# Where pieces of VectorE and ScalarE work end in the list of work of a two-layer perceiver kernel

## The chip, the cores and the metric

The kernel runs on one core of one Trainium2 chip. The metric is the device time of one launch in microseconds (us), the median of several runs. A profiled execution of the kernel gives the durations below; it is one execution, with a time of its own.

## What is computed

The input x has 16 sequences of 64 tokens of 256 numbers; a context has 16 sequences of 1601 rows of 256. Six blocks follow each other, each on a normed x and added to it (types are float32 throughout):

```
x = x + cross_attention_0(layernorm(x), ctx)       # softmax(QK/16) V, then an output matrix
x = x + self_attention(layernorm(x))               # 16 heads of 16, low rank, q and k normed by their root mean square, causal
x = x + tiled_ffn(layernorm(x))                    # one of 8 matrices by position
x = x + cross_attention_1(layernorm(x), ctx)
x = x + state_space(layernorm(x))                  # convolution, softplus time steps, scan over 64 tokens, gate
x = x + experts(layernorm(x))                      # 8 of 64 experts a token, plus one shared
```

layernorm is (x - mean) / sqrt(var + 1e-5) over the 256 numbers.

## The kernel before, in words

The 1024 tokens lie in SBUF as 8 groups g of 128 (two sequences each). The blocks are folded into one program with these stages:

- **Attention stage.** chain(g) does for one group the query and cross attention of layer 0 ("a"), mla (self attention), ffn, and cross attention of layer 1 ("b"). Before a cross, turn_ctx transposes the context of a sequence (on TensorE, copied to cT). At the end prepare_ssm loads and transposes W_in for the next block.
- **State space and routing stage.** inlet(g) makes the convolution and its transposes, sums(lo, hi) the softplus and its segment sums, which go through DRAM (segd), scan(g) the scan, route(g) the choice of experts; the chosen rows are scattered by GpSimd into a table in DRAM, xbuf, sorted by expert.
- **Expert stage.** Rows come back by quads of experts (L1442), pass up and down, and are scattered by GpSimd into a second table in DRAM, ybuf, one row for each token and choice (L1481). At the end each group reads its 8 rows a token from ybuf (L1555) and sums them with their weights.

**What sets the order.** The stages are generators, and drive (a planner in the program text) lets several run at once: two chains at a time, and beside them one prepare_ssm, two inlets, one sums. Each `yield cost, gap` tells the planner that the step just written takes TensorE `cost` us and that the generator should not go on for `gap` us more; the planner takes the first generator whose time has come. A third word may stand there: "want" asks for the one slot for attention scores, "free" gives it up. The order of the text so made is a priority for the framework that builds the program: it puts the instructions of each engine in an order of its own, by when they become ready and by that priority, and each engine executes its own order strictly.

Places that the change and the later steps touch:

- layernorm, L199 to L214: bn_stats (L201), bn_aggr (L203) and the sum with epsilon ve (L205) on VectorE, the power -0.5 rs on GpSimd (L207), the apply xn on VectorE (L213). All are written at once, and after it the caller yields (0, 2.7) or the like. In query of layer a, `beside` is turn_ctx of the group's first context: its seven steps stand between the norm and the transposes of xn.
- turned, L658: two transposes of xn, then a copy of them (xnT) by evac, L190, which takes VectorE (L195) and ScalarE (L197) in turns over all its calls.
- cross, L562: scores in four pieces j (L576), each with its maximum (L583); exponentials on ScalarE (L597), then `yield 0.3, 2.0, "free"`. After it come the sum and its reciprocal (L601, L603), turn(j), which transposes a piece (L612) and copies it to paT by evac, and weigh, the product with the context (L620).
- mla, L742: products with q and k weights (mq, L753) and their squares on ScalarE (L754); the root of the mean square on VectorE, one sum, two small operations and three rounds of three (L757 to L767), and q and k times it (mqk, L773). Then a copy of xnT by GpSimd (L780), v (mv, L783), its masked form vb (L785), transposes and keys (L796 to L806), "want", and the scores in four tiles pss (L819). The softmax runs in two halves i, both written in one step: mask added (L830, two), maximum (L837), difference (L838), exponential mee on ScalarE (L840). After the two halves `yield 1.2, 3.8, "free"`, then transposes (L846), copies (L848) and the product with v (L856).
- clear, L183: called by chain(g) after mla(g); two transfers on SP's queue that wait for mla's last product write an eighth of xbuf (L185) and an eighth of ybuf (L187) with zeros from a small tile, each row in two halves of 136 or 128 numbers. load_ctx (L379, L380) and W_in's tiles wl (L997, L1000) use the same queue.
- sums, L309: softplus in some 24 small VectorE operations (L320 to L338) around one exponential (L322), written in one step.
- inlet, ffn and route call layernorm as the others do.

Of the kernel before, what the change touches and what calls it, by code (L numbers as in the profile page):

```python
# [10 lines left out]
F32 = mybir.dt.float32  # L11
I32 = mybir.dt.int32
# [6 lines left out]
P = 128  # L19
# [128 lines left out]
def perceiver_kernel(ctx: ExitStack, tc: tile.TileContext, a: dict, consts: bass.AP, out: bass.AP):  # L148
# [28 lines left out]

    zero = cst.tile([P, DX // 2], F32, name="zero")
    G.memset(zero, 0.0)
    xbuf0 = xbuf.rearrange("(p n) (c d) -> p (n c) d", p=P, c=2)  # L180
    ybuf0 = ybuf.rearrange("(p n) (c d) -> p (n c) d", p=P, c=2)

    def clear(lo, hi, stage):  # L183

        after(nc.sync.dma_start(out=xbuf0[:, 2 * lo : 2 * hi, :], in_=_bc(zero, 1, 2 * (hi - lo))), [stage])  # L185
        lo, hi = (n * NTOK * TOPK // NSLOT for n in (lo, hi))
        after(nc.sync.dma_start(out=ybuf0[:, 2 * lo : 2 * hi, :], in_=_bc(zero[:, 0 : D // 2], 1, 2 * (hi - lo))), [stage])  # L187

# [9 lines left out]

    def layernorm(src, name, xn, parted=False):  # L199
        st = small.tile([P, 6], F32, tag="ln_st", name=f"st_{name}")  # L200
        V.bn_stats(st, src)  # L201
        mv = small.tile([P, 2], F32, tag="ln_mv", name=f"mv_{name}")
        V.bn_aggr(mv, st)  # L203
        ve = small.tile([P, 1], F32, tag="ln_ve", name=f"ve_{name}")
        V.tensor_scalar(ve, mv[:, 1:2], 1e-5, None, ALU.add)  # L205
        rs = small.tile([P, 1], F32, tag="ln_rs", name=f"rs_{name}")
        G.tensor_tensor(rs, ve, neghalf[:, 0:1], ALU.pow)  # L207
        if parted:

            src, to = src.rearrange("p (k c) -> p k c", c=2), xn.rearrange("p (c k) -> p k c", c=2)  # L210
        else:
            to = xn
        V.tensor_scalar(to, src, mv[:, 0:1], rs, ALU.subtract, ALU.mult)  # L213
        return xn  # L214

# [51 lines left out]
    def inlet(g, tile1, tile2):  # L267
        yield from until(lambda: "winT" in sw)
        xnT, winT = sw["xnT"], sw["winT"]
        tk = slice(g * P, (g + 1) * P)  # L270
        xn = layernorm(x[:, g, :], f"ss{g}", tile1([P, D], f"xn_ss{g}"))
        yield 0, 2.8
        pt = pst([P, 2, P], f"psx_ss{g}")
# [35 lines left out]
    def sums(lo, hi):  # L309
# [11 lines left out]
        u = sp("u")  # L321
        A.activation(u, na, AF.Exp)  # L322
        up2 = sp("up2")
        V.tensor_scalar(up2, u, 2.0, None, ALU.add)
# [8 lines left out]
        for k in range(13, 0, -2):  # L333
            V.tensor_tensor(po, po, r2, ALU.mult)
            V.tensor_scalar(po, po, 2.0 / k, None, ALU.add)
        V.tensor_tensor(po, po, r, ALU.mult)
        dt = sp("dt")
        V.scalar_tensor_tensor(dt, dv, 0.0, po, ALU.max, ALU.add)  # L338
        yield 0, 4.0
        sg = sw["pool"].tile([n, (NL + 1) * P], F32, tag="sg", name=f"sg_{lo}")  # L340
# [10 lines left out]
    with ExitStack() as p1:  # L351
# [181 lines left out]
        def query(g, lay, beside=None):  # L533
# [3 lines left out]
            xs = x[:, g, :]  # L537
            xn = layernorm(xs, f"xa{nm}", tile1([P, D], f"xn_{nm}"))
            if beside:
                yield from beside  # L540
            else:
                yield 0, 2.7
            xnT = turned(xn, f"xa{nm}")
# [18 lines left out]
        def cross(g, lay):  # L562
# [31 lines left out]
            for j in range(4):  # L594
# [3 lines left out]
                pas.append(pa)  # L598
            yield 0.3, 2.0, "free"
            sm = small.tile([P, 1], F32, tag="sm", name=f"sm_{nm}")  # L600
# [141 lines left out]
        def mla(g):  # L742
            wqk, wvo, wkr, vbs = wts["m"]
            xs = x[:, g, :]
            xn = layernorm(xs, f"ml{g}", tile1([P, D], f"xn_ml{g}"))
            yield 0, 2.7
            xnT = turned(xn, f"ml{g}")
# [3 lines left out]
            for c in range(2):  # L751
# [3 lines left out]
                pqs.append(pq)  # L755
            ms = small.tile([P, 32], F32, tag="mms", name=f"mms_{g}")
            V.reduce_sum(ms, sq.rearrange("p c (n d) -> p (c n) d", d=HD), AX.X)  # L757
            me = small.tile([P, 32], F32, tag="mme", name=f"mme_{g}")
            V.tensor_scalar(me, ms, 1.0 / HD, EPS_RMS, ALU.mult, ALU.add)

            rr = small.tile([P, 32], F32, tag="mrr", name=f"mrr_{g}")
            V.tensor_scalar(rr.bitcast(I32), me.bitcast(I32), -0.5, 1597463007.0, ALU.mult, ALU.add)
            for i in range(3):
                t = small.tile([P, 32], F32, tag="mt", name=f"mt_{g}_{i}")
                V.tensor_tensor(t, rr, rr, ALU.mult)
                V.scalar_tensor_tensor(t, t, -0.5, me, ALU.mult, ALU.mult)
                V.scalar_tensor_tensor(rr, t, 1.5, rr, ALU.add, ALU.mult)  # L767
            qk = tile2([P, 2, 2, P], f"mqk_{g}")
            for c in range(2):
                pv = pqs[c].rearrange("p (j n d) -> p j n d", j=3, d=HD)  # L770
                rv = rr.rearrange("p (c j n) -> p c j n", c=2, j=2)
                for j in range(2):
                    V.tensor_tensor(  # L773
                        qk[:, c, j, :].rearrange("p (n d) -> p n d", d=HD), pv[:, 2 * j, :, :], _bc(rv[:, c, j, :], 2, HD), ALU.mult
                    )
            yield 0.7, 0.1
            vs = []
            for c in range(2):
# [12 lines left out]
                vs.append(vb)  # L791
            yield 0.9, 5.0
            ptq = pst([P, 2, P], f"mtq_{g}")
# [22 lines left out]
            for c in range(2):  # L816
                for r in range(4):
                    for b in range(2):
                        T.matmul(  # L819
                            pss[r][b * 64 : (b + 1) * 64, c, :],  # L820
                            lhsT=qT[r * 32 : (r + 1) * 32, c, b * 64 : (b + 1) * 64],
                            rhs=kbs[c][r * 32 : (r + 1) * 32, b, :, :].rearrange("p h k -> p (h k)"),
                            start=True,
                            stop=True,
                        )
            ees, eTs = [], []
            for i in range(2):
# [13 lines left out]
                ees.append(ee)  # L841
            yield 1.2, 3.8, "free"
            for i in range(2):
# [87 lines left out]
        def ffn(g):  # L931
            fw, ohb, fb = wts["f"]
            xs = x[:, g, :]
            xn = layernorm(xs, f"ff{g}", tile1([P, D], f"xn_ff{g}"))
            yield 0, 2.7
            xnT = turned(xn, f"ff{g}")
# [192 lines left out]
    def route(g):  # L1129
# [5 lines left out]
        tk = slice(g * P, (g + 1) * P)  # L1135
        layernorm(x[:, g, :], f"mo{g}", xr[:, g, :], parted=True)
        yield 0, 2.8 if g == NG - 1 else 5.0
        pt = pst([P, 2, P], f"psx_mo{g}")
# [497 lines left out]
```

## Time and profile before

| | us |
|---|---|
| runs, device time | 1113.68, 1114.81, 1122.16 |
| median | 1114.81 |
| profiled execution, device time | 1104.11 |
| its span, first to last instruction | 1102.2 |

| stage (us from the span's start) | TensorE busy | VectorE busy | ScalarE busy | GpSimd busy | granted clock |
|---|---|---|---|---|---|
| 0 to 602, attention | 495.8 | 290.8 | 150.7 | 44.0 | 0.92 |
| 602 to 644, inlets | 26.2 | 30.5 | 18.2 | 8.2 | 0.80 |
| 644 to 890, scan and routing | 202.7 | 182.2 | 51.7 | 126.8 | 0.76 |
| 890 to 1062, experts | 159.2 | 68.4 | 50.6 | 91.5 | 0.96 |
| 1062 to 1102, sum of the rows | 17.3 | 18.5 | 0.0 | 3.9 | 0.78 |

The granted clock is TensorE's, as a share of full speed. In the profile's lines PE is TensorE, PEld its weight load, DVE VectorE, ACT ScalarE, POOL GpSimd, SPq the DMA queue of SyncE; L12 is line 12 of the kernel, and the names are those of the program, out<-in. In a timeline a line begins with its start and its duration in us; what stands in brackets at its end is the idle time of the engine before it and what ended that. A wait for several things is put down to the one that came last.

### The profile page before, as it was taken

The page shows a single profiled execution, that of the slowest core. Times are in us where ns is not written, and L with a number is a line of the kernel's source. Part 1 is how long each engine was busy: PE and PEld are TensorE (multiplying, and loading weights), DVE is VectorE, ACT ScalarE, POOL GpSimd, SP SyncE. Part 2 cuts the span into 40 slices and gives each one's busy share as a digit, 9 for nine tenths or more (in the row PEclk, how much of TensorE's full clock was granted, in tenths as well). Part 3 has the DMA queues.
Part 4 walks back from the last instruction along what each step waited for, and adds up shares of the span by engine and source line. Part 5 has one row for each costly group of instructions (what it writes and reads, how often), then busy time and mean ns, then how long its engine had stood idle before and what let it go on. Part 6 is the DMA issues. An engine that isn't in the chain of part 4 may idle for free. (4 is left out here: it accounts for less than half of the span.)

```text
span 1102.2 us, 16572 instructions
## 1 busy us (share of the span) xinstructions
PE 901.2 (82%) x6242; PEld 684.8 (62%) x6242; DVE 590.5 (54%) x1823; ACT 271.2 (25%) x592; POOL 274.4 (25%) x326
## 2 busy tenths in 40 slices
PE   4887889978799788979867569999999449999955
PEld 3665656645656456556554458888888338888834
DVE  1346454356545554364535874976867773343316
ACT  0213132321332222331313543222210013233310
POOL 0000101001000001001010222266665524655650
PEclk7878998989999899999978878887867669999988
DMA  6411324303613307103430073544411877989336
GB/s 235 172 38 62 100 89 130 120 2 99 184 36 120 97 4 219 59 2 100 103 91 11 28 153 84 118 113 113 113 42 41 277 263 241 304 282 296 116 119 269
DMA packets 99511, 138.99 MB, mean 126 GB/s; under 512 B 10211, under 2 KB 85407, under 8 KB 96358
## 3 DMA queue, kind: packets, MB, share of 16 engines
q1 hardware_dynamic: 84816, 116.36, 34.8%
q0 software_dynamic: 7680, 17.33, 4.6%
q10 hardware_dynamic: 6934, 4.23, 1.5%
q8 instruction: 50, 0.82, 0.3%
q14 instruction: 31, 0.25, 0.1%
HBM read 97.54 MB, written 44.53 MB: 129 GB/s over the span
## 5 line engine op out<-in xcount | busy, mean ns | idle before, releaser
L1481 POOL DMA_INDIRECT ybuf<-yo,goal x96 | 93.5, 974 | 81.3 <-ACT yo L1507 32.7
L1473 PE MATMUL ps_ee<-xT,wq 128*128 128x192 f32 x512 | 96.1, 331 | 0.0
L1115 POOL DMA_INDIRECT xbuf<-xtok,idx x64 | 70.0, 1094 | 71.3 <-DVE idx L1205 48.1
L1473 PEld LDWEIGHTS ps_ee<-xT,wq 128*128 128x128 f32 x512 | 82.5, 191 | 6.5 <-issue 5.0
L620 PE MATMUL po_a<-cn,paT_a 128*64 128x256 f32 (+1 forms) x416 | 59.5, 424 | 22.6 <-ACT mee L840 19.2
L207 POOL TENSOR_TENSOR rs_ff<-ve_ff,neghalf 128x1 f32<-128x1 f32 x8 | 4.4, 548 | 219.1 <-DVE ve_ff L205 211.6
L946 PE MATMUL fpy<-fw,fxm 128*128 128x256 f32 x256 | 58.3, 387 | 0.7 <-DVE fxm L943 0.7
L1337 PEld LDWEIGHTS ps_g<-pc,pb 64*128 64x128 f32 x768 | 51.8, 207 | 10.4 <-issue 5.1
L620 PE MATMUL po_b<-cn,paT_b 128*64 128x256 f32 (+1 forms) x416 | 51.2, 395 | 7.9 <-DVE paT_b L195 4.5
L1337 PE MATMUL ps_g<-pc,pb 64*128 64x64 f32 x768 | 54.7, 295 | 3.0 <-DVE zt L1326 2.0
L620 PEld LDWEIGHTS po_a<-cn,paT_a 128*64 128x64 f32 (+1 forms) x416 | 31.0, 150 | 40.9 <-ACT mee L840 20.1
L946 PEld LDWEIGHTS fpy<-fw,fxm 128*128 128x128 f32 x256 | 49.3, 196 | 8.8 <-PE py_a L654 2.2
L391 PE MATMUL psc<-ct,cn 128*128 128x128 f32 x384 | 52.3, 289 | 2.8 <-DVE cc_a L558 2.8
L391 PEld LDWEIGHTS psc<-ct,cn 128*128 128x128 f32 x384 | 46.9, 150 | 6.6 <-DVE cc_a L558 3.1
L576 PE MATMUL sc_a<-cT,qT_a 128*64 128x512 f32 (+1 forms) x256 | 48.7, 521 | 0.0
L1461 PE MATMUL ps_xT<-ct,xg 128*128 128x128 f32 x192 | 30.9, 289 | 19.7 <-DMA xg<-xbuf 19.7
L1323 POOL TENSOR_TENSOR pc<-cT,e 128x256 f32<-128x256 f32 x48 | 36.1, 787 | 39.3 <-ACT cT L1306 39.3
L1347 DVE COPY_PREDICATED gt<-ct,ps_g 128x256 f32<-128x256 uint32 x96 | 42.3, 545 | 5.2 <-PE ps_g L1337 5.2
L576 PE MATMUL sc_b<-cT,qT_b 128*64 128x512 f32 (+1 forms) x256 | 44.7, 501 | 0.4
L197 ACT COPY cT<-psc 128x512 f32<-128x512 f32 x48 | 28.0, 589 | 66.5 <-PE psc L391 66.5
L620 PEld LDWEIGHTS po_b<-cn,paT_b 128*64 128x64 f32 (+1 forms) x416 | 28.8, 141 | 24.9 <-DVE paT_b L195 5.5
L1475 ACT ACTIVATE hg<-ps_ee 128x192 f32<-128x192 f32 x64 | 21.2, 331 | 93.6 <-PE ps_ee L1473 90.9
(430 smaller groups left out, 1831.9 us busy)
## 6 DMA issues: line engine op xcount, KB each, us to landing
cn<-in_ctx_dram SPq DMA_DIRECT2D x16, 1536.0 KB
e<-segd SPq DMA_DIRECT2D x16, 896.0 KB
xbuf<-zero SPq DMA_DIRECT2D x8, 1632.0 KB
xg<-xbuf SPq DMA_DIRECT2D x16, 816.0 KB
ybuf<-zero SPq DMA_DIRECT2D x8, 1024.0 KB
wq<-in_L_ffn_We_gate_dram SPq DMA_DIRECT2D x16, 512.0 KB
wq<-in_L_ffn_We_up_dram SPq DMA_DIRECT2D x16, 512.0 KB
wq<-in_L_ffn_We_down_dram SPq DMA_DIRECT2D x16, 512.0 KB
```

The source lines that it names most:

```text
L197: A.copy(dst, src)
L391: T.transpose(ps[:, j, :], cn[:, 4 * q + j, c * P : (c + 1) * P], ident)
L576: T.matmul(sc[b * 64 : (b + 1) * 64, :], lhsT=qT[:, c, b * 64 : (b + 1) * 64], rhs=cTs[2 * g + b][:, c, 512 * j : 512 * j + n], start=c == ...
L620: T.matmul(po[b * 64 : (b + 1) * 64, :], lhsT=paTs[j][:, i, b * 64 : (b + 1) * 64], rhs=cns[2 * g + b][0:r, k, :], start=k == 0, stop=k == KC,
L946: T.matmul(py, lhsT=xm[:, t, c, :], rhs=fw[:, 2 * h + t, c, :], start=h + t + c == 0, stop=h == 3 and t == 1 and c == 1,)
L1115: sct = G.indirect_dma_start(out=xbuf, out_offset=bass.IndirectOffsetOnAxis(ap=idx[:, g, k : k + 1], axis=0), in_=xtok[:, g, 0:DX], in_off ...
L1323: G.tensor_tensor(pc[:, l, :, :].rearrange("p j (k h) -> p j k h", h=1 << l), half(cT, l, 1), half(ev, l, 1), ALU.mult)
L1337: T.matmul(pgs[q][:, i, j, :], lhsT=pb[q * 64 : (q + 1) * 64, l + i, j, :], rhs=pc[q * 64 : (q + 1) * 64, l + i, j, :], start=True, stop=True,
L1347: V.copy_predicated(gt.rearrange("p (j q) (k u h) -> p q j k u h", q=2, u=2, h=h)[:, q, :, :, 1, :], _bc(lvl[:, l + i, :].rearrange("p (k ...
L1461: T.transpose(to, xgs[q][:, 2 * part + s, c * P : (c + 1) * P], ident)
L1473: T.matmul(pe[:, j, :], lhsT=w, rhs=xTs[q][:, i, c, :], start=c == 0, stop=c == 1)
L1481: arr = G.indirect_dma_start(out=ybuf, out_offset=bass.IndirectOffsetOnAxis(ap=goal, axis=0), in_=y, in_offset=None, bounds_check=NTOK * T ...
```

## The change

- layernorm becomes a generator. After rs it yields (0, 1.8), or, where `beside` is given, three steps of it; then the apply is written, and then the rest of `beside`. The callers yield (0, 0.9) behind it instead of (0, 2.7) (route: 1.0 or 3.2 instead of 2.8 or 5.0).
- mla: v and vb are written ahead of the root; yields stand between the root and mqk, between the scores and the softmax, and between the softmax's halves. The score slot is given up after the second half, as before.
- cross: copies of the pieces go to VectorE for even j and to ScalarE for odd j; the yield before them is (0.35, 2.4).
- sums: three yields more.
- clear: xbuf is cleared with whole rows of 272 numbers; ybuf is not cleared.

```diff
-    zero = cst.tile([P, DX // 2], F32, name="zero")
+    zero = cst.tile([P, DX], F32, name="zero")
     G.memset(zero, 0.0)
-    xbuf0 = xbuf.rearrange("(p n) (c d) -> p (n c) d", p=P, c=2)
-    ybuf0 = ybuf.rearrange("(p n) (c d) -> p (n c) d", p=P, c=2)
+    xbuf0 = xbuf.rearrange("(p n) d -> p n d", p=P)
     def clear(lo, hi, stage):
-        after(nc.sync.dma_start(out=xbuf0[:, 2 * lo : 2 * hi, :], in_=_bc(zero, 1, 2 * (hi - lo))), [stage])
-        lo, hi = (n * NTOK * TOPK // NSLOT for n in (lo, hi))
-        after(nc.sync.dma_start(out=ybuf0[:, 2 * lo : 2 * hi, :], in_=_bc(zero[:, 0 : D // 2], 1, 2 * (hi - lo))), [stage])
+        after(nc.sync.dma_start(out=xbuf0[:, lo:hi, :], in_=_bc(zero, 1, hi - lo)), [stage])
...
-    def layernorm(src, name, xn, parted=False):
+    def layernorm(src, name, xn, parted=False, beside=None):
...
         G.tensor_tensor(rs, ve, neghalf[:, 0:1], ALU.pow)
+        if beside is None:
+            yield 0, 1.8
+        else:
+            for _ in range(3):
+                yield next(beside)
...
         V.tensor_scalar(to, src, mv[:, 0:1], rs, ALU.subtract, ALU.mult)
-        return xn
+        if beside is not None:
+            yield from beside
...
@@ sums
         A.activation(u, na, AF.Exp)
+        yield 0, 1.2
...
             V.tensor_scalar(po, po, 2.0 / k, None, ALU.add)
+            if k in (9, 5):
+                yield 0, 1.2
...
-        yield 0, 4.0
+        yield 0, 1.5
@@ query, and likewise inlet, mla, ffn and route without beside
-            xn = layernorm(xs, f"xa{nm}", tile1([P, D], f"xn_{nm}"))
-            if beside:
-                yield from beside
-            else:
-                yield 0, 2.7
+            xn = tile1([P, D], f"xn_{nm}")
+            yield from layernorm(xs, f"xa{nm}", xn, beside=beside)
+            if not beside:
+                yield 0, 0.9
@@ cross
-            yield 0.3, 2.0, "free"
+            yield 0.35, 2.4, "free"
...
-                evac(paT, pt)
+                (A.copy if j % 2 else V.tensor_copy)(paT, pt)
@@ mla
                 pqs.append(pq)
-            ms = small.tile([P, 32], F32, tag="mms", name=f"mms_{g}")
...
-                    V.tensor_tensor(
-                        qk[:, c, j, :].rearrange("p (n d) -> p n d", d=HD), pv[:, 2 * j, :, :], _bc(rv[:, c, j, :], 2, HD), ALU.mult
-                    )
-            yield 0.7, 0.1
+            yield 1.0, 0
             vs = []
...
                 vs.append(vb)
-            yield 0.9, 5.0
+            yield 0.9, 0.3
+            ms = small.tile([P, 32], F32, tag="mms", name=f"mms_{g}")
...
+                V.scalar_tensor_tensor(rr, t, 1.5, rr, ALU.add, ALU.mult)
+            yield 0, 2.8
+            qk = tile2([P, 2, 2, P], f"mqk_{g}")
...
+            yield 0, 1.2
             ptq = pst([P, 2, P], f"mtq_{g}")
...
+            yield 0.7, 0.2
             ees, eTs = [], []
...
                 ees.append(ee)
-            yield 1.2, 3.8, "free"
+                yield (0, 2.0) if i == 0 else (0, 1.0, "free")
             for i in range(2):
...
-                yield 0.55, (1.3, 0.7)[i]
+                yield 0.55, (1.5, 0.7)[i]
```

More of the change, by code (lines that the diff above doesn't have):

```diff
@@ L270, in inlet @@
         tk = slice(g * P, (g + 1) * P)
-        xn = layernorm(x[:, g, :], f"ss{g}", tile1([P, D], f"xn_ss{g}"))
-        yield 0, 2.8
+        xn = tile1([P, D], f"xn_ss{g}")
+        yield from layernorm(x[:, g, :], f"ss{g}", xn)
+        yield 0, 0.9
         pt = pst([P, 2, P], f"psx_ss{g}")
@@ L537, in query @@
             xs = x[:, g, :]
-            xn = layernorm(xs, f"xa{nm}", tile1([P, D], f"xn_{nm}"))
-            if beside:
-                yield from beside
-            else:
-                yield 0, 2.7
+            xn = tile1([P, D], f"xn_{nm}")
+            yield from layernorm(xs, f"xa{nm}", xn, beside=beside)
+            if not beside:
+                yield 0, 0.9
             xnT = turned(xn, f"xa{nm}")
@@ L744, in mla @@
             xs = x[:, g, :]
-            xn = layernorm(xs, f"ml{g}", tile1([P, D], f"xn_ml{g}"))
-            yield 0, 2.7
+            xn = tile1([P, D], f"xn_ml{g}")
+            yield from layernorm(xs, f"ml{g}", xn)
+            yield 0, 0.9
             xnT = turned(xn, f"ml{g}")
@@ L755, in mla @@
                 pqs.append(pq)
-            ms = small.tile([P, 32], F32, tag="mms", name=f"mms_{g}")
[L757 to L772, printed above, removed]
-                    V.tensor_tensor(
-                        qk[:, c, j, :].rearrange("p (n d) -> p n d", d=HD), pv[:, 2 * j, :, :], _bc(rv[:, c, j, :], 2, HD), ALU.mult
-                    )
-            yield 0.7, 0.1
+            yield 1.0, 0
             vs = []
@@ L791, in mla @@
                 vs.append(vb)
-            yield 0.9, 5.0
+            yield 0.9, 0.3
+            ms = small.tile([P, 32], F32, tag="mms", name=f"mms_{g}")
+            V.reduce_sum(ms, sq.rearrange("p c (n d) -> p (c n) d", d=HD), AX.X)
+            me = small.tile([P, 32], F32, tag="mme", name=f"mme_{g}")
+            V.tensor_scalar(me, ms, 1.0 / HD, EPS_RMS, ALU.mult, ALU.add)
+            rr = small.tile([P, 32], F32, tag="mrr", name=f"mrr_{g}")
+            V.tensor_scalar(rr.bitcast(I32), me.bitcast(I32), -0.5, 1597463007.0, ALU.mult, ALU.add)
+            for i in range(3):
+                t = small.tile([P, 32], F32, tag="mt", name=f"mt_{g}_{i}")
+                V.tensor_tensor(t, rr, rr, ALU.mult)
+                V.scalar_tensor_tensor(t, t, -0.5, me, ALU.mult, ALU.mult)
+                V.scalar_tensor_tensor(rr, t, 1.5, rr, ALU.add, ALU.mult)
+            yield 0, 2.8
+            qk = tile2([P, 2, 2, P], f"mqk_{g}")
+            for c in range(2):
+                pv = pqs[c].rearrange("p (j n d) -> p j n d", j=3, d=HD)
+                rv = rr.rearrange("p (c j n) -> p c j n", c=2, j=2)
+                for j in range(2):
+                    V.tensor_tensor(
+                        qk[:, c, j, :].rearrange("p (n d) -> p n d", d=HD), pv[:, 2 * j, :, :], _bc(rv[:, c, j, :], 2, HD), ALU.mult
+                    )
+            yield 0, 1.2
             ptq = pst([P, 2, P], f"mtq_{g}")
@@ L933, in ffn @@
             xs = x[:, g, :]
-            xn = layernorm(xs, f"ff{g}", tile1([P, D], f"xn_ff{g}"))
-            yield 0, 2.7
+            xn = tile1([P, D], f"xn_ff{g}")
+            yield from layernorm(xs, f"ff{g}", xn)
+            yield 0, 0.9
             xnT = turned(xn, f"ff{g}")
@@ L1135, in route @@
         tk = slice(g * P, (g + 1) * P)
-        layernorm(x[:, g, :], f"mo{g}", xr[:, g, :], parted=True)
-        yield 0, 2.8 if g == NG - 1 else 5.0
+        yield from layernorm(x[:, g, :], f"mo{g}", xr[:, g, :], parted=True)
+        yield 0, 1.0 if g == NG - 1 else 3.2
         pt = pst([P, 2, P], f"psx_mo{g}")
```

## The prediction

> **What bounds the kernel now.** I read the page's slices first, then the busy time by stage, then the waits of TensorE up to 602 us, and last the timeline around each long wait.
>
> ```profile
> PE   4887889978799788979867569999999449999955
> PEclk7878998989999899999978878887867669999988
> ```
>
> No engine is full from end to end. By stage (busy time by windows): four fifths of the attention stage, 0 to 602 us, is TensorE work (495.8 us); the short stage from 602 to 644 us is VectorE (30.5 of 42 us, TensorE 26.2); 644 to 890 us is TensorE (202.7) and VectorE (182.2) together; 890 to 1062 us is TensorE alone (159.2 of 172). The change lies almost wholly in the first stage, so what counts there is when TensorE stands still:
>
> ```profile
> PE po_a L620 <- ACT mee L840: 19.2, 4, 4.8
> PE pq_a L550 <- DVE xnT_xaa L195: 8.5, 3, 3.1
> PE ps_win L1041 <- DMA wl<-in_L_attn_W_in_dram: 7.8, 1, 7.8
> ```
>
> The columns are total us, times, longest. Three causes, eight stalls, 35.5 us. The timeline of the first (one of four alike, near 105, 235, 363 and 491 us):
>
> ```profile
> 363.62 0.68 DVE L837 TENSOR_REDUCE mmx<-ms 128x8 f32<-128x512 f32 x1
> 364.32 0.69 DVE L838 TENSOR_TENSOR ms<-ms,mmx 128x512 f32<-128x512 f32 x1
> 364.93 0.75 DVE L830 TENSOR_TENSOR ms<-ms,ct 128x256 f32<-128x256 f32 x2
> 365.72 0.69 DVE L837 TENSOR_REDUCE mmx<-ms 128x8 f32<-128x512 f32 x1
> 366.44 0.69 DVE L838 TENSOR_TENSOR ms<-ms,mmx 128x512 f32<-128x512 f32 x1
> 367.05 0.68 DVE L195 COPY paT_a<-pspa_a 128x512 f32<-128x512 f32 x1
> 367.88 3.40 PE L620 MATMUL po_a<-cn,paT_a 128*64 128x256 f32 x16 [4.81 <-ACT mee L840]
> ```
>
> The reader is to see a queue. TensorE ended the transposes pspa_a at 363.07; the copy paT_a that the next matmuls need was therefore ready to start. It stood on VectorE behind both halves of self attention's softmax and ran at 367.05. The wait is booked to ScalarE's mee only because that ended at about the same time.
>
> The second cause (three times, near 164, 294 and 421 us) is a norm in front of a copy:
>
> ```profile
> 164.50 0.15 DVE L205 TENSOR_SCALAR ve_ff<-mv_ff 128x1 f32<-128x1 f32 x1
> 165.38 0.80 DVE L213 TENSOR_SCALAR xn_ff<-x,mv_ff,rs_ff 128x256 f32<-128x256 f32 x1 [0.73 <-POOL rs_ff L207]
> 166.10 0.41 DVE L195 COPY xnT_xaa<-psx_xaa 128x256 f32<-128x256 f32 x1
> 166.57 2.07 PE L550 MATMUL pq_a<-xnT_xaa,pr_A 128*128 128x128 f32 x8 [2.70 <-DVE xnT_xaa L195]
> ```
>
> VectorE waits 0.73 us for the power on GpSimd, applies the norm, and only then copies what TensorE has waited for since 163.87. The third is a transfer behind a transfer on SP's queue:
>
> ```profile
> 547.22 4.83 SPq L187 DMA_DIRECT2D ybuf<-zero  x1
> 552.10 5.70 SPq L1000 DMA_DIRECT2D wl<-in_L_attn_W_in_dram  x4
> 559.21 1.94 PE L1041 MATMUL ps_win<-ct,wl 128*128 128x128 f32 x8 [7.83 <-DMA wl<-in_L_attn_W_in_dram]
> ```
>
> One more thing must be known: the order on an engine is not the order in which the code is written. Inside one step of mla the copies of the other chain stand between the steps of the root:
>
> ```profile
> 351.70 0.18 DVE L765 TENSOR_TENSOR mt<-mrr 128x32 f32<-128x32 f32 x1
> 351.80 0.69 DVE L195 COPY cT<-psc 128x512 f32<-128x512 f32 x1
> 352.40 0.18 DVE L766 SCALAR_TENSOR_TENSOR mt<-mt,mme 128x32 f32<-128x32 f32 x1
> ```
>
> So the builder already fills holes, and what a yield changes is which of two ready instructions goes first. That is just what fails in the first two causes.
>
> **The change part by part.** *Self attention's softmax, and the engines of the copies.* By the yields: the crossing chain ends its scores at t, gives up its slot at t+0.35 and turns its first piece at t+2.75. mla issues its scores at t+0.35, half 0 at t+1.25, half 1 at t+3.25, which the 0.55 of turn(0) pushes to 3.3. The order becomes half 0, paT of piece 0 on VectorE, half 1; piece 1 goes to ScalarE, where in time it is ready before half 1's exponential. In the trace's times: L830 twice ends at 361.36, mmx and ms of half 0 (0.68 + 0.69) at 362.8, the sum sm_a waits as now for the exponentials until 363.54 and with the reciprocal ends at 363.9, the copy (0.68) at 364.6, TensorE starts at 364.7 instead of 367.88: 3.2 us, four times, **-12.8**. What is late next is half 1: its exponential ends about 367.2 (364.6 + 0.75 + 0.69 + 0.69 + 0.63), about as now (367.85), so mla's own chain loses nothing by this sum. The copies themselves: piece 3 was copied by VectorE for layer b (L195 paT_b, mean 480 ns, two forms) and now goes to ScalarE, with the 512-wide pieces shared; 8 x (687 - 290) ns = 3.2 us more on VectorE and less on ScalarE, in a stage where VectorE is busy 290.8 of 602 us: nothing on the path. Mla now keeps the score slot until half 1 is issued, 2.9 of planned time instead of 1.2. Who waits for that? The next cross scores (L576) start 34 to 36 us after mla's scores (L819) in every pair I looked at (101.5 to 138.0, 147.2 to 181.0, 360.0 to 395.2): nobody.
>
> *Self attention's root.* mv and vb are issued ahead of it and the root is cut from mqk. At 349.7 to 355 us the two already stand mixed and TensorE is full (9.98 of 10 us): 0. Uncovered, it could move mqk by two vb, 0.84 us, on eight mla.
>
> *Norms.* L213 is issued 1.8 of planned time later. Near 164 us the copy xnT_xaa can then follow ve_ff directly at 164.65 and ends at 165.06 instead of 166.51: 1.45 us, three times, **-4.4**. The apply then waits for rs_ff to 165.34 as before and is at most 0.1 us later. Other norms: xtok L213 leaves VectorE idle 19.0 us in all for rs_mo in the scan stage (a reading of the groups), where copies into gt could go first; TensorE's waits for psx_mo there are only 8 us in all, so I take **-2** between 0 and -8. In the last route the apply could be late by one small operation: +0.2 us, up to +1.
>
> *Zeros of ybuf.* Eight transfers of 1024 KB go. Between 550 and 558 us the engines moved 284 to 333 GB/s, so 1.05 MB is 3.5 us; the clear of xbuf with rows of 1088 bytes instead of two of 544 is worth up to 1 us. [...] I take 0.7. Seven of the eight clears are hidden: TensorE waits for no cn at all in the list. The eighth stands in front of wl: wl lands 4.2 us earlier, and the 7.83 us stall becomes 3.6: **-4.2**. If prepare_ssm should issue those wl ahead of the clear, more; if later work stops TensorE there instead, 0.
>
> *Softplus.* Same instructions, three places to be interrupted, planned 1.1 longer in sum. Its two uses bound a TensorE wait of 3.77 us (L343 on sp_dt, near 658) and lie beside VectorE-bound conv work (9.76 and 9.62 of 10 us from 610 to 630): 0, between -3 and +3.
>
> *The clock.* After long stalls the granted clock is 0.5. Windows behind the stalls show it:
>
> ```profile
> 364.00:371.00 7.00, 3.12 (x16) 1.91 (x16) 3.66 (x8) 1.74 (x3) 0.00 (x0) 0.51 0.00 0
> 166.00:173.00 7.00, 6.43 (x29) 6.32 (x30) 2.90 (x7) 1.23 (x3) 0.76 (x2) 0.51 1.11 295
> 294.00:301.00 7.00, 3.85 (x31) 3.62 (x31) 4.42 (x11) 1.36 (x4) 1.97 (x3) 1.00 1.10 303
> ```
>
> (The seventh number is the clock.) TensorE work under the slow clock behind the stalls: 17.5 us behind the four softmax stalls, 9.7 behind two of the three norms, 2.9 behind wl; together 30 us, half of it lost, 15 us. [...] The rows do not agree: a stall of 2.70 us (163.87) was followed by the slow clock and one of 3.15 us (294.05) was not. Since 1.67 us more of idleness stands just ahead of each softmax stall, I take half: **-7.5**, ends 0 and -15.
>
> *Against it.* Every step of mla is now open to the other chain, and TensorE executes in order, so a step placed too early blocks it. By the sum above half 1's exponential ends at 367.2 and its transposes (L846) come up on TensorE at about 367.3: no margin. I take 1 us for each of eight mla: **+8**, between 0 and +36 (see below).
>
> Sum: -12.8 - 4.4 - 2 + 0.2 - 4.2 - 7.5 + 8 = -22.7. The profiled execution took 1104.11 us (span 1102.2 and 1.9 around it), so 1081.4. The median of the runs shown is 1114.81, 1.0097 times that; 1081.4 x 1.0097 = **1091.9**, say 1092.
>
> **The rivals.** *Only the zeros count (0.2).* The builder fills holes by itself, so the finer steps merely exchange one copy for another, and the four stalls of 4.8 us come back elsewhere. For it: the mixed order shown above. Against it: the copy paT_a was ready and still went last. Then -4.2 and a little clock, -1.4: 1098.5, as a median 1109.
>
> *Everything comes (0.08).* No new stall and the whole clock: -12.8 - 4.4 - 4 - 4.2 - 15 = -40: 1064, as a median 1074.
>
> *The stall moves to half 1 (0.12), slower.* TensorE reaches L846 of half 1 before its exponential. A full half and its exponential cost 0.75 + 0.69 + 0.69 + 0.63 = 2.8 us, and 3.4 us of slow clock behind it lose 1.7: 4.5 on eight mla is +36; the softmax gain is then void, with norms and zeros -8.6 kept: +27, 1131.5, as a median 1142. It decides over the gain from about (22.7 + 8) / 8 = 3.8 us each. For it: no margin in the sum. Against it: today the other chain puts eight to sixteen matmuls between the two L846.
>
> **How the numbers follow.** The likeliest (0.6) is 1092, its own range 1078 to 1104 (ends of the clock, of the new stalls and of the scan). Under 1073 lie about 0.05 (part of the second rival), over 1113 about 0.15 (the third, and the edge of the first), so 1073 to 1113 holds 8 in 10. One per cent, about what a measurement of this kernel can tell from none, is 11 us: faster means under 1103.7. Faster: most of the likeliest and the whole second rival, 0.68; same 0.2, nearly all from the first; slower 0.12.
>
> **What would show it.** Right: L620 waits of about 1.5 us instead of 4.8 on four places, paT_a between the two pairs of L830 on VectorE; pq_a waiting about 1.2 us; ps_win about 3.6 us; fewer half-clock stretches before 602 us and a stage that ends some 20 us earlier; the scan and expert stages as long as now. Wrong: new waits of TensorE at L846 or for mee of half 1, equal stalls at other lines, or a scan stage that grows by more than 5 us from its changed order.

## The result, and the profile after

The changed kernel takes 1146.4 us, the median of four runs (1144.07 to 1146.86), beside 1116.9 for the kernel before on the same chip: a ratio of 1.0276 (95% interval 1.0243 to 1.0309). It is slower. (The experiments ran on other chips, where the kernel before takes 1105.4 to 1106.7 us; so each is told as a ratio to before on its own chip.) Its profiled execution took 1144.07 us (span 1142.3), 40 us more than that of before (1104.11, span 1102.2).

The first thing to read is the slices of the page, the share of TensorE's work and its granted clock, in 40 equal parts of the span:

```profile
PE   4887888987999889888878568898999539999945
PEclk8879988989999899898978888677777569999978
```

TensorE looks as busy as before. The loss has to be looked for by stages. They are cut at events that both traces have (the first score product sc_a, the last po_b, the first and the last expert product ps_ee). "Half clock" is the time for which the trace's clock record holds half speed, whether TensorE works or not; "stalls" are TensorE's idle times above 1.5 us.

| | attention: length | idle | stalls, their sum | half clock, stretches | state space to routing: length | half clock |
|---|---|---|---|---|---|---|
| before | 557.7 | 88.8 | 14, 47.9 | 78.5, 11 | 301.4 | 148.6 |
| after | 580.0 | 84.8 | 26, 59.8 | 119.5, 22 | 311.7 | 163.8 |

Of the 40 us, 22.3 lie in the attention stage and 10.3 in the next; the start, the experts and the tail bring 2.6, 2.2 and 2.6. In the attention stage TensorE is not idle for longer. Its work takes longer, and the same work is done. The windows of that stage show it, before and after (columns: length, then busy time and count of TensorE, its weight loads, VectorE, ScalarE, GpSimd, then the granted clock):

```profile
42.80:600.40 557.60, 468.75 (x3436) 316.66 (x3435) 280.03 (x807) 143.83 (x340) 41.56 (x77) 0.93 0.28 87
```

```profile
45.00:627.00 582.00, 497.21 (x3464) 334.57 (x3463) 284.79 (x813) 142.11 (x344) 42.01 (x78) 0.90 0.19 69
```

The reader is to see 468.8 us of TensorE work become 497.2 with a clock of 0.90 instead of 0.93 (495.2 at the borders of the table; the second window ends 1.5 us later). Counted is the work done under half clock, without the idle time under it: 53.3 us before, 106.1 after. (Sixteen products of po's form take 3.40 us under it in the kernel before, at 367.88, and 1.95 at full clock, at 199.75.) Half of the 52.8 us more is 26.4, and the work grew by just that; 4.0 us less of idle time leave the 22.3. The sum holds in all sixteen traces of this document: TensorE's own work in this stage (added idle products left out), less half of what ran at half clock, is 441.4 to 446.2 us, and 442.2 in both before and after.

Why the clock fell is in the list of what TensorE waited for in the changed kernel (total, times, longest, us):

```profile
PE pspa_a L619 <- ACT pa_a L604: 14.0, 7, 2.4
PE pspa_b L619 <- ACT pa_b L604: 11.7, 5, 2.4
PE po_a L627 <- ACT mee L851: 10.3, 4, 2.7
PE psx_xab L669 <- DVE xn_b L216: 7.8, 3, 2.6
PE pq_a L557 <- DVE xnT_xaa L192: 6.0, 3, 2.0
```

The stalls of 4.8 and 7.8 us are gone, as meant. In their place stand shorter ones: 19 of 2 to 2.85 us, where the kernel before had 4. Two of these rows are new in kind, psx_xab behind the norm xn_b and the longer pspa_b. The timeline of the changed kernel around one of them shows what is missing there:

```profile
141.79 0.19 DVE L792 SCALAR_TENSOR_TENSOR mrr<-mt,mrr 128x32 f32<-128x32 f32 x1
141.92 0.69 DVE L590 TENSOR_REDUCE mx_b<-sc_b 128x1 f32<-128x512 f32 x1
...
145.35 0.82 DVE L590 TENSOR_REDUCE mx_b<-sc_b 128x1 f32<-128x512 f32 x2 [1.02 <-PE sc_b L583]
...
147.88 1.97 PE L619 MATMUL pspa_b<-ct,pa_b 128*128 128x128 f32 x8 [2.35 <-ACT pa_b L604]
149.03 0.69 DVE L621 COPY paT_b<-pspa_b 128x512 f32<-128x512 f32 x1 [2.17 <-PE pspa_b L619]
149.84 0.28 DVE L799 TENSOR_TENSOR mqk<-mq,mrr 128x128 f32<-128x128 f32 x1
155.11 2.38 PE L627 MATMUL po_b<-cn,paT_b 128*64 128x256 f32 x20
157.42 0.44 PE L806 MATMUL mtq<-ct,mqk 128*128 128x128 f32 x2
160.99 0.69 PE L829 MATMUL ms<-mkb,mqT 32*64 32x128 f32 x32
```

and the same place in the kernel before:

```profile
138.50 0.88 DVE L773 TENSOR_TENSOR mqk<-mq,mrr 128x128 f32<-128x128 f32 x4
139.96 0.69 DVE L583 TENSOR_REDUCE mx_b<-sc_b 128x1 f32<-128x512 f32 x1 [0.57 <-PE sc_b L576]
143.51 0.44 PE L796 MATMUL mtq<-ct,mqk 128*128 128x128 f32 x2
145.87 0.66 PE L612 MATMUL pspa_b<-ct,pa_b 128*128 128x128 f32 x4 [1.03 <-ACT pa_b L597]
146.46 0.69 PE L819 MATMUL ms<-mkb,mqT 32*64 32x128 f32 x32
```

Before, mqk stood on VectorE ahead of the other chain's score maxima mx_b; its turned form mtq and self attention's scores ms then fell into the hole between sc_b and the exponentials. After, the root is ready at 141.98, but mqk stands in VectorE's order behind the maxima and behind the first copy paT_b, and VectorE has to wait for sc_b and the exponentials before it gets there. So mqk starts 9.9 us after sc_b's start (139.93) instead of 0.5 (137.97), mtq stands on TensorE behind the whole po_b, and ms runs 15.5 us after sc_b's end instead of 2.9. The hole stays empty. All four such places of the stage are alike.

What followed this stall is in the windows just behind it (the seventh number is the clock):

```profile
144.70:148.10 3.40, 1.05 (x13) 0.62 (x10) 1.41 (x5) 1.14 (x3) 0.00 (x0) 0.97 0.00 0
148.10:151.50 3.40, 3.40 (x18) 2.37 (x19) 1.70 (x7) 2.22 (x7) 0.00 (x0) 0.53 0.03 5
151.50:154.90 3.40, 3.40 (x31) 1.88 (x27) 0.69 (x1) 0.00 (x0) 0.00 (x0) 1.00 0.00 0
```

The stall fills most of the first window; the next runs at 0.53, the one after that at full clock again.

### The profile page after: what moved, and what is told of

It reads as the page before. It is cut to its first block, busy times and chain, and to the rows that moved or that the text cites. A ratio compares the mean times of both kernels' runs of the same rounds, so it can differ in the third digit from the quotient of the medians.

```text
span 1142.3 us, 16570 instructions
## 1 busy us (share of the span) xinstructions
PE 929.5 (81%) x6242; PEld 701.6 (61%) x6242; DVE 598.5 (52%) x1823; ACT 263.7 (23%) x592; POOL 273.0 (24%) x326
## 5 line engine op out<-in xcount | busy, mean ns | idle before, releaser
L627 PE MATMUL po_a<-cn,paT_a 128*64 128x256 f32 (+1 forms) x416 | 64.4, 434 | 10.5 <-ACT mee L851 10.3
L958 PE MATMUL fpy<-fw,fxm 128*128 128x256 f32 x256 | 61.5, 401 | 0.9 <-DVE fxm L955 0.9
L958 PEld LDWEIGHTS fpy<-fw,fxm 128*128 128x128 f32 x256 | 51.6, 203 | 11.3 <-issue 2.4
L627 PE MATMUL po_b<-cn,paT_b 128*64 128x256 f32 (+1 forms) x416 | 56.5, 414 | 0.0
L583 PE MATMUL sc_b<-cT,qT_b 128*64 128x512 f32 (+1 forms) x256 | 48.0, 530 | 0.0
L1473 PE MATMUL ps_xT<-ct,xg 128*128 128x128 f32 x192 | 30.5, 287 | 19.5 <-DMA xg<-xbuf 19.5
L205 POOL TENSOR_TENSOR rs_ml<-ve_ml,neghalf 128x1 f32<-128x1 f32 x8 | 4.4, 548 | 158.2 <-DVE ve_ml L203 158.2
L627 PEld LDWEIGHTS po_b<-cn,paT_b 128*64 128x64 f32 (+1 forms) x416 | 31.2, 149 | 17.8 <-issue 5.1
```

Of the source, the lines that this page charges most:

```text
L583: T.matmul(sc[b * 64 : (b + 1) * 64, :], lhsT=qT[:, c, b * 64 : (b + 1) * 64], rhs=cTs[2 * g + b][:, c, 512 * j : 512 * j + n], start=c == ...
L627: T.matmul(po[b * 64 : (b + 1) * 64, :], lhsT=paTs[j][:, i, b * 64 : (b + 1) * 64], rhs=cns[2 * g + b][0:r, k, :], start=k == 0, stop=k == KC,
L958: T.matmul(py, lhsT=xm[:, t, c, :], rhs=fw[:, 2 * h + t, c, :], start=h + t + c == 0, stop=h == 3 and t == 1 and c == 1,)
L1473: T.transpose(to, xgs[q][:, 2 * part + s, c * P : (c + 1) * P], ident)
```

## The experiments

**Theory A**: the finer steps of self attention put the two chains out of step, the holes stay unfilled, and each brings half clock. **Theory B**: the norms' yields did it. **Theory C** (from the ninth run on): the slow clock, not the idle time, is the loss. The first eight take over single parts of the change.

**e1, self attention alone**: v ahead of the root, and its yields.

```diff
+            yield 0, 2.8
             qk = tile2([P, 2, 2, P], f"mqk_{g}")
...
+            yield 0, 1.2
             ptq = pst([P, 2, P], f"mtq_{g}")
...
+            yield 0.7, 0.2
             ees, eTs = [], []
...
-            yield 1.2, 3.8, "free"
+                yield (0, 2.0) if i == 0 else (0, 1.0, "free")
```

> Kernel before with the self attention part of the change alone (v ahead of the root, root cut from mqk, softmax in two steps). Theory A, mla's finer steps let the other chain's cross go first, so that mqk and mla's scores come some 10 us later, two chains fall out of step and TensorE has more stalls of 2 to 3 us, each followed by a stretch at half clock: this part alone carries most of the loss, 20 to 32 us slower than before, half-clock time before the last cross up from 78 us to 110 or more. Theory B, the loss comes from the norms' later apply: within 5 us of before, or faster by up to 13 us by the softmax sum.

Measured 1138.2 us, 1.0312 (1.0262 to 1.0362): the whole loss, and more. TensorE shows the changed kernel's order and stalls: psx_xab 2.59, pspa_b 2.35, pq_a 2.00, po_a 2.70; mqk starts 10.3 to 10.6 us after sc_b's start, and the attention stage has 116.1 us of half clock.

**e2, the norms alone**, in all callers.

```diff
         G.tensor_tensor(rs, ve, neghalf[:, 0:1], ALU.pow)
+        if beside is None:
+            yield 0, 1.8
...
-            yield 0, 2.7
+            yield 0, 0.9
```

> Kernel before with the norms alone as generators. Theory A: within 6 us of before, if anything faster, since three stalls of 2.7 us shrink to about 1.3. Theory B (the norms' applies come late and every chain waits for them): 15 to 30 us slower, with new waits of TensorE for xn.

Measured 1100.4 us, 0.9957 (0.9930 to 0.9985). The norms help; theory B falls. The attention stage is 549.1 us, with 64.9 us of half clock, and the waits of pq_a fall from 8.5 us in sum to 3.9.

**e3, the crossing chain alone.**

```diff
-            yield 0.3, 2.0, "free"
+            yield 0.35, 2.4, "free"
-                evac(paT, pt)
+                (A.copy if j % 2 else V.tensor_copy)(paT, pt)
```

> Kernel before with the fixed engines for the copies of the attention pieces and the yield of (0.35, 2.4) alone. Both theories: within 5 us of before. If a third holds, that the longer yield or the turns of the other copies put the chains out of step: over 10 us slower.

Measured 1129.2 us, 1.0204 (1.0161 to 1.0247). Neither A nor B had this. Its timeline shows a queue like that of po_a before, in a new place, four times:

```profile
153.01 0.69 DVE L837 TENSOR_REDUCE mmx<-ms 128x8 f32<-128x512 f32 x1
153.73 0.69 DVE L838 TENSOR_TENSOR ms<-ms,mmx 128x512 f32<-128x512 f32 x1
154.34 0.68 DVE L614 COPY paT_b<-pspa_b 128x512 f32<-128x512 f32 x1
155.17 3.39 PE L620 MATMUL po_b<-cn,paT_b 128*64 128x256 f32 x16 [4.63 <-ACT mee L840]
```

The later turn puts self attention's scores ahead of pspa_b, and so both halves of its softmax ahead of the copy that po_b needs.

**e4, the zeros alone.**

```diff
-        after(nc.sync.dma_start(out=xbuf0[:, 2 * lo : 2 * hi, :], in_=_bc(zero, 1, 2 * (hi - lo))), [stage])
-        after(nc.sync.dma_start(out=ybuf0[:, 2 * lo : 2 * hi, :], in_=_bc(zero[:, 0 : D // 2], 1, 2 * (hi - lo))), [stage])
+        after(nc.sync.dma_start(out=xbuf0[:, lo:hi, :], in_=_bc(zero, 1, hi - lo)), [stage])
```

> Kernel before with the zeros of ybuf gone and xbuf cleared by whole rows, nothing else. Both theories: 3 to 8 us faster, the wait of ps_win for wl down from 7.8 us to about 3.6. If this wait is of no consequence: within 2 us.

Measured 1102.6 us, 0.9954 (0.9932 to 0.9976). The wait for wl, 7.8 us before, in its list of waits:

```profile
PE ps_win L1038 <- DMA wl<-in_L_attn_W_in_dram: 4.6, 2, 3.7
```

**e5, the softmax's halves alone, and e6, v ahead of the root with its two yields alone.**

```diff
# e5
+            yield 0.7, 0.2
-            yield 1.2, 3.8, "free"
+                yield (0, 2.0) if i == 0 else (0, 1.0, "free")
-                yield 0.55, (1.3, 0.7)[i]
+                yield 0.55, (1.5, 0.7)[i]
# e6, behind the root and behind mqk
+            yield 0, 2.8
-            yield 0.9, 5.0
+            yield 0, 1.2
```

> Kernel before with the softmax in two steps alone (the yields between scores and softmax, between the halves and behind them); root and v as before. If the root's cut from mqk does the harm of self attention's part, this alone is 5 to 15 us faster than before, with the stalls of po_a down from 4.8 us to 2.7 and mla's second scores still next to the other chain's (some 3 us behind sc_b). If the two steps do it: 15 us or more slower.

> Kernel before with v written ahead of the root and the root cut from mqk, softmax as before. If the root's cut does the harm: 20 to 35 us slower, mqk standing behind the other chain's score maxima on VectorE and the second mla's scores 15 us later than sc_b's end instead of 3; the stalls of po_a stay at 4.8 us where they occur. Else: within 5 us of before.

e5: 1107.9 us, 1.0010 (0.9985 to 1.0034). e6: 1108.9 us, 1.0036 (1.0006 to 1.0066). Each alone costs nothing or 0.4%; both together, e1, cost 3.1%. e6 alone puts mqk behind the other chain's score maxima, 6.9 us after sc_b's start, and ms 5.1 us after its end; only both together put it behind the copy paT_b as well. e5's list of waits holds the stall that was shortened and the one that came:

```profile
PE psx_xab L662 <- DVE xn_b L213: 10.6, 4, 2.8
PE po_a L620 <- ACT mee L841: 10.4, 4, 2.7
```

TensorE is idle for 72.1 us instead of 88.8 in e5's attention stage, but 79.1 us of its work ran at half clock instead of 53.3, and the stage is only 2.9 us shorter.

**e7, fixed engines alone** (the second pair of e3's lines).

> Kernel before with the fixed engines for the copies of pieces alone, yield (0.3, 2.0) kept. If VectorE's copy of piece 0 behind the softmax makes the new stall of po_b (4.6 us, four times, clock behind it): 15 to 25 us slower. If the yield of (0.35, 2.4) makes it: within 5 us of before.

Measured 1112.3 us, 1.0064 (1.0045 to 1.0082): a stall of 2.0 us at po_b, four times. The attention stage is 3.5 us longer than before here and 13.0 us in e3, so most of e3's loss there came with its yield. In both traces the stage behind it is some 8.5 us longer too, though all four engines execute it in the order of before; the last section comes back to this.

**e8, norms and zeros** (the diffs of e2 and e4).

> Kernel before with the two parts that gained alone, norms as generators and the clear without ybuf, together. If the parts add: ratio 0.991, about 9 to 10 us faster than before. If they share a gain: 5 us.

Measured 1098.7 us, 0.9935 (0.9912 to 0.9958): below both kernels; the gain is a little less than that of the two apart (0.9957 x 0.9954 = 0.991).

**e9, one number.** e1, with

```diff
-                yield (0, 2.0) if i == 0 else (0, 1.0, "free")
+                yield (0, 2.0) if i == 0 else (0, 2.1, "free")
```

> Self attention's part of the change alone, with one number altered: the planned gap after the second half of its softmax is 2.1 instead of 1.0. In TensorE's program this puts self attention's turned queries and its scores back right behind sc_b, as in the kernel before; nearly all else stands as in the kernel with self attention's part alone. Theory A (the loss comes from self attention's steps standing behind the other chain's whole po_b, so that nothing fills that chain's waits): the stalls of 2.6 us at psx_xab and 2.35 us at pspa_b go, four times each, some 20 us and the slow clock behind them; those at po_a and pspa_a stay. Ratio to before 1.000 to 1.015. Rival (the pieces themselves cost, wherever they stand): 1.025 to 1.035, as without the altered number.

Measured 1108.8 us, 0.9981 (0.9945 to 1.0018): the loss of 3.1% is gone. The timeline has mtq behind sc_b again and ms ahead of po_b:

```profile
145.12 0.82 DVE L583 TENSOR_REDUCE mx_b<-sc_b 128x1 f32<-128x512 f32 x2 [1.02 <-PE sc_b L576]
146.56 0.87 DVE L791 TENSOR_TENSOR mqk<-mq,mrr 128x128 f32<-128x128 f32 x4
146.89 0.33 PE L798 MATMUL mtq<-ct,mqk 128*128 128x128 f32 x1 [1.59 <-DVE mqk L791]
148.12 1.04 PE L612 MATMUL pspa_b<-ct,pa_b 128*128 128x128 f32 x8
150.38 0.72 PE L821 MATMUL ms<-mkb,mqT 32*64 32x128 f32 x32 [1.22 <-ACT paT_b L197]
151.03 1.95 PE L620 MATMUL po_b<-cn,paT_b 128*64 128x256 f32 x16
```

On VectorE mqk still stands behind the maxima mx_b, 6.9 us after sc_b's start as in e6, but ahead of the first copy paT_b. So the wait for the maxima is not what costs. The windows of the attention stage, e1 and then e9:

```profile
44.00:627.00 583.00, 495.28 (x3440) 329.53 (x3440) 282.86 (x812) 142.76 (x341) 41.87 (x78) 0.90 0.26 83
```

```profile
47.00:602.00 555.00, 473.98 (x3446) 319.55 (x3444) 282.89 (x811) 142.49 (x340) 42.06 (x78) 0.94 0.27 86
```

Idle time fell by only 7 us (87.7 to 81.0), TensorE's work by 22.2 (495.9 to 473.7 at the table's borders), of which 56.7 us ran at half clock instead of 101.3 (half of 44.6 is 22.3). The pieces are the same in both. Where they stand makes the difference, and it is paid through the clock.

**e10, two numbers.** e9, with

```diff
-            yield 0, 2.8
+            yield 0, 2.0
             qk = tile2([P, 2, 2, P], f"mqk_{g}")
```

> Self attention's part alone, with two numbers altered (2.1 as above, and 2.0 instead of 2.8 after the root): TensorE's order in the attention stage is then nearly that of the kernel before, while root, products, halves and all other steps stay cut as in the change. Theory A: 0.995 to 1.005 of before, with the po_a stall near 2.7 us instead of 4.8. Rival (finer pieces cost by themselves): above 1.02.

Measured 1098.2 us, 0.9921 (0.9882 to 0.9961), better than theory A had it. With the order of before nearly restored (mqk 0.8 us after sc_b's start), the finer pieces bring what they were made for: attention 539.1 us, stalls of 25.9 us in sum, half clock 59.3.

**e11, idle products in the changed kernel.**

```diff
+                if j == 0:
+                    for _ in range(7):
+                        T.matmul(pt[:, 0, :], lhsT=ident, rhs=ident, start=True, stop=True)
```

in turn, and the same ahead of the first weigh of every other layer-a cross and ahead of four psx_xab.

> The changed kernel with idle work for TensorE put where it stands still: seven products of the identity by itself (128x128, into a tile that is overwritten right after) before the first turned piece of each crossing group, before the first po_a of every other group and before four psx_xab, 24 times some 1.8 us, 44 us of added matmuls. Theory C (most of the stage's loss is the half clock behind stalls of 2 to 2.7 us): half-clock time in the attention stage falls from 119 us to under 80, and the time falls by 5 to 20 us in spite of the added work: ratio to before 1.010 to 1.023. Rival (the stalls themselves are the loss, the clock is a follower of no weight): the added work overruns the stalls here and there and the ratio is 1.03 to 1.05, whatever the clock.

Measured 1113.0 us, 1.0034 (1.0000 to 1.0069), against 1.0276 without them: 43.4 us of added work in the trace, and the kernel is some 27 us faster. The window of its attention stage:

```profile
47.60:595.80 548.20, 498.25 (x3782) 346.83 (x3781) 283.87 (x810) 139.89 (x341) 42.00 (x78) 0.96 0.20 72
```

Half clock fell from 119.5 to 38.5 us. Of the kernel's own work 30.5 us ran under it instead of 106.1, and this work fell from 495.2 to 459.8 us; the added products lie in the stalls (idle 50.0 instead of 84.8). One thing is not the same: the framework moved mq ahead of psx_xab in four places, which fills that hole too.

**e12, the whole change with e9's number** (the diff of e9 on the changed kernel).

> The whole change, with the one number altered (2.1 instead of 1.0 after the second half of self attention's softmax), which puts self attention's turned queries and scores back behind sc_b. Theory A: 1.000 to 1.015 of before. Rival (the cross chain's own part, 1.020 alone, is a second cause of equal weight): 1.018 to 1.030.

Measured 1120.6 us, 1.0109 (1.0074 to 1.0144). The order takes 1.6% off. What remains over e9 is 1.0109 / 0.9981 = 1.013 though norms and zeros are in it (0.991): 1.022 for the rest. That is near e3's 1.020, but e3's stalls of 4.6 us at po_b are not in this trace, nor in the changed kernel's. Its attention stage is 7.9 us longer than e9's with the same idle time (80.3 and 81.0): 72.2 us of its work ran at half clock instead of 56.7. The stage behind it is 5.5 us longer. Which of the other parts does this, no run separates.

**e13, idle products in the kernel before**, at an otherwise unchanged order of TensorE: 6 ahead of the first pspa_a and 12 ahead of the second, in the four groups with the longest stall.

```diff
+                if j < 2 and lay == "a" and g % 2 == 1:
+                    for _ in range((6, 12)[j]):
+                        T.matmul(pt[:, 0, :], lhsT=ident, rhs=ident, start=True, stop=True)
```

> The kernel before with 18 idle products of the identity by itself (128x128) in each of its four longest double stalls: 6 ahead of the first turned piece pspa_a, 12 between it and the second, ahead of po_a. TensorE's order is otherwise the same, nothing of the change is in it; 72 products of some 0.26 us are 19 us of added work. Theory C (the half clock behind the stalls is a loss of its own): half-clock time in the attention stage falls from 78 us to about 60, and the time by 5 to 9 us: 0.992 to 0.996. Rival (the stalls alone count, the clock is a follower without weight): the products lie inside the stalls and change nothing, or overrun them: 1.000 to 1.008.

Measured 1102.1 us, 0.9962 (0.9938 to 0.9986). Its timeline at one such place:

```profile
232.72 1.60 PE L613 MATMUL pspa_a<-ct 128*128 128x128 f32 x12 [1.67 <-ACT pa_a L597]
234.16 0.60 PE L615 MATMUL pspa_a<-ct,pa_a 128*128 128x128 f32 x4
234.60 2.84 PE L613 MATMUL pspa_a<-ct 128*128 128x128 f32 x24
237.28 0.60 PE L615 MATMUL pspa_a<-ct,pa_a 128*128 128x128 f32 x4
238.95 1.95 PE L623 MATMUL po_a<-cn,paT_a 128*64 128x256 f32 x16 [1.07 <-ACT mee L843]
```

From the first pspa_a to po_a it is 6.2 us, as before: the products are hidden, and po_a takes 1.95 us instead of 3.40. Half clock is 64.9 us instead of 78.5. Theory C has its sign, at the edge of its range, and the rival's 1.000 and more is outside the interval. But much of the half clock that went lay over idle time: 49.7 us of the kernel's own work ran under it instead of 53.3, and the profiled attention stage is only 0.7 us shorter. So the size rests on the runs.

**e14, what helped, together**: the diffs of e10, e4 and e13, the last with (6, 8).

> What the runs point to as a best version: self attention's part with the two altered gaps (2.1 and 2.0), ybuf left unfilled, and 14 idle products in each of the four double stalls that are left there (6 ahead of the first pspa_a, 8 ahead of the second). If the parts add (0.992 for the gaps, 0.995 for the zeros, 0.995 for the products): 0.980 to 0.986. If the clock's phase in the later stages takes it back: 0.987 to 0.995.

Measured 1078.1 us, 0.9736 (0.9707 to 0.9764), below both kernels and below the product of the parts (0.9921 x 0.9954 x 0.9962 = 0.984). Attention takes 530.4 us with 37.5 of half clock. The stage behind it takes 301.1 us, where e10's profiled execution had 311.2 in the same order on all four engines. That is about the difference, and it may be luck of the clock (see the last section).

## Why the prediction was wrong

It said 1092 and faster; the kernel took 1146.4. The step that failed is the second, "*Self attention's root* ... 0", with its reason that mv, vb and the root "already stand mixed and TensorE is full". It priced the yields behind the root apart from those of the softmax, as a change within self attention's own chain (0.84 us at most). Each of the two alone does cost little; together they cost 3.1%. The runs show where the cost begins, alike at all four places of each trace:

| | mqk after sc_b's start, us | ms after sc_b's end, us | ratio |
|---|---|---|---|
| before | 0.5 | 2.9 | 1 |
| e5, softmax's yields | 2.6 | 2.9 | 1.0010 |
| e6, root's yields | 6.9 | 5.1 | 1.0036 |
| e1, both | 10.3 to 10.6 | 17.3 to 18.2 | 1.0312 |
| e9, both, gap 2.1 | 6.9 | 5.1 | 0.9981 |
| whole change | 9.9 | 15.5 to 16.4 | 1.0276 |
| e12, whole change, gap 2.1 | 6.9 | 5.1 | 1.0109 |

Behind the other chain's score maxima alone, mqk is 6.4 us late and little is lost: mtq still comes up on TensorE ahead of pspa_b. With the first copy paT_b ahead of it too, it waits for the exponentials and for pspa_b, and mtq and ms fall behind the whole po_b. So 1.6 of the 2.8% hang on this order (e12); for the rest the points below give what is known, and part of it stays open. The prediction took a yield to decide only "which of two ready instructions goes first"; in the changed kernel VectorE stood idle for 1.02 us ahead of a maximum, twice, and for 2.17 ahead of paT_b, with mqk ready behind them. TensorE kept its order in the same way: in the kernel before it stood idle until 367.88, ahead of po_a, though mee of half 0 was there from 365.68; the transposes mpe of it stood behind po_a and ran at 371.20.

The prediction's own caution, "a step placed too early blocks it", was put on one place only, half 1 at L846, and priced there at +8 (its sum for half 1, 367.2, comes to 367.4); the wait for mee of half 1 is 1.2 us at most. The rival that named 1142 was near by accident, since its mechanism did not happen.

Point by point:

- **Softmax, -12.8.** Direction right: paT_a stands between the halves. The stall is 2.69 us, not 1.5, since the sum sm_a stands ahead of half 0's maximum, not behind it, and holds VectorE until the last exponential:

```profile
108.82 0.16 DVE L608 TENSOR_REDUCE sm_a<-sm_a 128x1 f32<-128x4 f32 x1 [2.24 <-ACT pa_a L604]
108.89 0.68 DVE L848 TENSOR_REDUCE mmx<-ms 128x8 f32<-128x512 f32 x1
109.61 0.69 DVE L849 TENSOR_TENSOR ms<-ms,mmx 128x512 f32<-128x512 f32 x1
110.21 0.68 DVE L621 COPY paT_a<-pspa_a 128x512 f32<-128x512 f32 x1
111.04 1.55 PE L627 MATMUL po_a<-cn,paT_a 128*64 128x256 f32 x6 [2.69 <-ACT mee L851]
```

  That is 8.5 us less of stalls, and in e5, which has no other part of the change, nothing of it is left: another stall, psx_xab, came with it, and more work ran at half clock.
- **Copy engines and the crossing chain's yield**, priced at nothing. e7: +0.6%; e3: +2.0%. I counted their load on the engines (3.2 us), not their place in the order. The stalls that they make alone are not in the changed kernel, so what they cost there is not shown.
- **Norms, -4.4 and -2, +0.2 for the last route**: right in e2 (-0.43%, 4.7 us; the waits of pq_a 4.6 us less). In the changed kernel these waits fell by 2.5 us only.
- **Zeros, -4.2**: right in e4. The stall of 7.8 became 3.7, where 3.6 was forecast; the gain was 5.1 us. No run shows the 0.7 us for whole rows of xbuf by itself: e4 has them together with the zeros of ybuf, 4.1 us less of this stall in all.
- **Softplus, 0**, between -3 and +3: no run of its own. Of the 10.3 us in the stage behind attention 7.7 are idle time, and four stalls, of 1.6, 1.7, 1.9 and 2.8 us (ps_yT twice, ps_sy, psx_mo), stand in the three traces of the changed kernel's kind (after, e11, e12) and in none of the other thirteen. The softplus's yields are the only part of the change that none of those has, so they are the likely cause, alone or with other parts. The prediction's own sign of being wrong, a scan stage over 5 us longer, came true.
- **The clock, -7.5**: the wrong sign. It was taken as a follower of the long stalls that go, over 30 us of work at half clock; in the whole stage this was 53.3 us and became 106.1, which lost 26.4 us. The half that it took of the 15 us was an estimate of its own. Of the stalls that it expected to remain, of about 1.5 us, most were free, as far as the traces show: in the attention stages of all sixteen, 42 of 148 stalls of 1.2 to 1.8 us had a half-clock stretch begin at them or within 2.5 us behind them. But of 80 stalls of 2.3 to 2.85 us 70 had one (before and after alone: 5 of 17, and 17 of 19; the last section says more).

## What to carry to other kernels

Where two chains fill each other's holes, a finer step is a change of order on every engine. Before pricing its duration, write down what the other chain can now put ahead of it, what that waits for, and which hole the delayed work used to fill. Count stalls by number and length, not by their sum: here the stalls of 4.8 and 7.8 us went, 19 of 2 to 2.85 us stood where there had been 4, and 106.1 us of work instead of 53.3 ran at half clock. And a planned gap is a number worth trying on its own: 1.0 or 2.1 at one place made 3% here.

## What the runs showed of the hardware

All 22 half-clock stretches in the changed kernel's attention stage last 3.41 us or 2 or 4 times that; one in the kernel before, at 425.47, also lasts 3.41. So a stall that brings one can cost 1.7 us (an estimate, half of 3.41, where TensorE works throughout), however short it is. The clock records of before and after show more: from end to end, every change of the clock lies a whole number of 3.4133 us from the others of its trace, to within 0.01 us.

What stood ahead of a fall can be counted when the traces are cut along these grids. All sixteen together have 235 windows at full clock in which TensorE worked for less than 40%; behind every one of them the clock fell. With 40 to 50% it fell behind 56 of 79, with more behind 150 of 3506. At half clock it never came back behind a window with less than 70% (427 of 427). In before and after alone it fell behind 35 of 35, 12 of 16 and 17 of 426, and did not come back in 55 of 55. By these counts a stall of some 2.1 us inside one window is enough (an estimate, 60% of 3.41), and a longer one that a border cuts may be none. Both cases are in the kernel before, in two stalls that the prediction names:

```profile
162.64:166.06 3.42, 1.23 (x13) 0.99 (x10) 2.66 (x7) 1.02 (x3) 1.27 (x3) 1.00 1.07 299
292.35:295.76 3.41, 1.70 (x16) 1.46 (x15) 2.82 (x8) 0.83 (x2) 0.34 (x1) 1.00 1.04 364
295.76:299.18 3.42, 1.98 (x18) 1.99 (x19) 1.63 (x4) 0.17 (x1) 1.63 (x3) 1.00 1.02 293
```

The stall of 2.70 us leaves 1.23 us of work in its window (36%), and half clock follows (0.50 from 166.06 to 169.47). The one of 3.15 us is cut by a border; its windows keep 50 and 58%, and the clock stays at 1.00.

Where the grid falls also goes together with about 9 us of the stage behind attention. In six traces all four engines execute this stage in the same order. In four of them (before, e4, e6, e13) the first border lies 2.5 to 3.1 us behind the last po_b, and it takes 300.7 to 301.9 us; in e3 and e7 it lies 0.9 us behind, and it takes 309.9 and 310.0. No run sets the grid, so it is not shown as a cause.

Work without use in the stalls raised the clock and shortened the kernel (half clock in the attention stage 119.5 to 38.5 us and 1.0276 to 1.0034 in e11, 78.5 to 64.9 and 0.9962 in e13), which I had not expected of a kernel whose TensorE is four fifths busy.
